# A grouped 3x3 convolution over normalised images: its beginning rearranged, and other work put between two PSUM writes

## The chip, the cores and the metric

The kernel runs on one core of a Trainium2 chip. The metric is the device time of one execution in microseconds (us): 1001.97 us before the change, the median of three runs that lay between 1000.68 and 1002.7 us.

The engines have short names in the profile. PE is TensorE (matrix products, results in PSUM), and PEld is its loading of weights. DVE is VectorE, ACT is ScalarE, POOL is GpSimd, and SP is the engine that issues most of the transfers. [...]

## The reference

The input `x` holds 160 images of 128 channels and 32 x 32 points in float32. There are five sets of weights, and each serves 32 of the images. Cut to what matters, the reference is:

```python
beta, alpha = jnp.max(U), jnp.min(U)
s1 = (beta - alpha) / 3.0
v1 = s1 * floor(U / s1)
s2 = s1 / 5.0
v2 = s2 * floor((U - v1) / s2)
w = (v1 + v2).reshape(128 * 5, 128, 3, 3)        # two-step quantised weights
g = _gn(x)                                       # 32 groups of 4 channels, per image
act = conv(g.reshape(32, 640, 32, 32), w, stride 1, pad 1, groups = 5)
return x + act.reshape(160, 128, 32, 32)
```

So every image needs a mean and a variance over each group of four channels, a normalised copy, a 3 x 3 convolution with quantised weights of its set, and the addition of the image itself.

## The kernel before

**One image is one step of the main loop** (`for i in range(self.imgs)` in `Main.run`), in which `conv(i)` is PE's part. A float32 image is represented by a high and a low float16 part, so that PE can work in float16. The 3 x 3 taps are split into three columns, worked in the order `COLS = (1, 0, 2)`. Rows are worked in pairs: the products of the sum and of the difference of two rows (`sums_of_pairs`) go to a PSUM tile `m`, of which there is only one, and the result rows to one of two PSUM tiles `eo`.

**The path of one image through the engines.** `measure(k, stages)` takes the sums (stage 0, line 192) and squares (stage 1, line 199) of an image that comes some ten to fifteen steps later; ACT does it, two passes an image, and for a few images (`by_vector`) DVE does it with `bn_stats` (line 182). When a group of images is measured, `means`, `deviations`, `variances`, `deviation` and `scales` turn that into factors, through two tiny PE products, small ACT copies and a chain on POOL. Images up to 6, and all even ones, are prepared by `normalise` and `high_part` on ACT (tiles `z`, `hi`; lines 510 and 518), `low_part` on DVE (`lo`, line 573) and `combinations` on DVE (`rows`, lines 587 to 590). The odd ones from 7 on are "combined": `outer_rows` on POOL and `combine` on DVE (tile `v`, lines 549 to 555) come first, `high_combined` on ACT (`vh`, line 560) and `low_combined` on DVE (`vl`, line 566) after that.

**Around one product of PE.** In `conv(i)`, PE first writes `m` for image i+1 (12 products if i+1 is combined, 6 if not), then the rest of image i into its `eo` tile. After the products into `m`, `leave(i+1)` copies one half of `m` to SBUF on ACT (line 708), and `pairs(i+1)` writes the sum (line 717) and then the difference (line 718) of the two halves into a fresh `eo`, both on DVE. Only when line 718 has read `m` may PE write `m` for the next image. `residual` (line 732) takes a finished `eo` out by ACT, and an accumulating transfer adds it to the image.

**The order of each engine's queue is written out by hand**: it is the order of the calls in `run`. The weights of the next set are quantised meanwhile in small steps on DVE: a generator `later`, of 14 instructions a column and three columns a set, from which `take(later, 1)` draws one instruction at a time; in an even step two are drawn (one after `low_part`, one after `pairs`), in an odd step one (after `low_combined`, ahead of `pairs`). A finished column is transposed by PE, and ACT makes `wt` and `half` of it (`keep_column`, lines 475 and 476).

**Ahead of the loop** stand the range of the weights, the quantising of the first set by columns (`first`, `second`, `third`), the statistics of images 0 to 7, and the direct products of images 0 to 2 (`direct_hi`, `direct_lo`, line 613), which don't use row pairs. `warm_up` gives PE ten products of zeros (line 631) while it waits.

**How far measuring runs ahead**: at step i, images up to `i + min(10 + i // 2, 15)` are measured. DVE measures the images 8, 10, 12, 14, 16 and 18.

Of the kernel before, what the change touches and what calls it, by code (L numbers as in the profile page):

```python
# [132 lines left out]
def run(steps):  # L133

    while True:
        try:
            next(steps)
        except StopIteration as end:
            return end.value
# [170 lines left out]
class Main:  # L310
# [24 lines left out]
    STAT_LEAD = 14  # L335
    LOAD_LEAD = 20
    STEADY = 7
    MEASURED = 20
    EARLY = 8
    FIRST = 3  # L340

# [4 lines left out]
    def __init__(self, tc, ctx, keep, x, u, out):  # L346
        nc = self.nc = tc.nc
        self.imgs, C, self.H, self.W = x.shape
        P = self.P = nc.NUM_PARTITIONS
        assert C == P and self.H * self.W == 1024  # L350
        self.per_set = self.imgs // N_SETS
        self.xv = x.rearrange("(b n) c h w -> n c b (h w)", n=N_SETS)
        self.ov = out.rearrange("(b n) c h w -> n c b (h w)", n=N_SETS)
        self.uv = u.rearrange("n (o i k) -> n o i k", o=C, k=TAPS)

        def pool(name, bufs, **kw):
            return ctx.enter_context(tc.tile_pool(name=name, bufs=bufs, **kw))

        self.const = pool("const", 1)
        self.qpool = pool("quant", 1)  # L360
        self.wpool = pool("weights", 2)
        self.upool = pool("u", 1)
        self.xpool = pool("x", 12)
        self.zpool = pool("z", 3)
        self.parts = pool("parts", 5)
        self.rows = pool("rows", 4)
        self.wide = pool("wide", 1)
        self.wide_parts = pool("wide_parts", 2)
        self.evac = pool("evac", 2)
        self.sums = pool("sums", 4)  # L370
        self.unread = pool("unread", 1)
        self.small = pool("small", 3)
        self.ps_eo = pool("ps_eo", 2, space=PSUM)
        self.ps_m = pool("ps_m", 1, space=PSUM)
        self.ps_stat = pool("ps_stat", 1, space=PSUM)
        self.ps_tr = pool("ps_tr", 1, space=PSUM)
        self.steps = Steps(nc, keep)
        self.chunks, self.z, self.hi, self.v, self.eo, self.m = {}, {}, {}, {}, {}, {}
        self.sum = {}
        self.wts = {}  # L380
        self.columns = []

        cuts = [0, 2, 4, 8, 12, *range(16, self.imgs + 1, 8)]
        self.groups = [range(a, b) for a, b in zip(cuts, cuts[1:])]
        self.group_of = {i: k for k, g in enumerate(self.groups) for i in g}
        self.stats = {}
# [95 lines left out]


    def by_vector(self, i):
        return self.EARLY <= i < self.MEASURED and i % 2 == 0

    def measure(self, i, stages=(0, 1)):

# [91 lines left out]
    def combinations(self, i):  # L580


        nc, P, H, W = self.nc, self.P, self.H, self.W
        lo = self.los[i % len(self.los)]
        rows = self.v[i] = self.rows.tile([P, 2048], MM, tag="rows", name=f"rows{i}")
        d, st = self.halves(rows)
        nc.vector.tensor_sub(d, lo[:, 0:H, :], lo[:, 2 : H + 2, :])
        pairs = lo[:, 1 : H + 1, :].rearrange("p (i a) w -> p a i w", a=2)
        nc.vector.tensor_add(st[:, 0], pairs[:, 0], pairs[:, 1])
        nc.vector.tensor_sub(st[:, 1], pairs[:, 1], pairs[:, 0])  # L590

    def halves(self, v):

# [28 lines left out]
    def banks(self, pool, tag, i):  # L622
        return pool.tile([self.P, 2, self.H // 2, self.W], F32, tag=tag, name=f"{tag}{i}")

    def warm_up(self):


        zeros = self.los[3].rearrange("p h w -> p (h w)")
        target = self.banks(self.ps_m, "m", "warm")
        for _ in range(10):  # L630
            self.nc.tensor.matmul(
                target[:, 0].rearrange("p i w -> p (i w)"), zeros[:, :128], zeros[:, :512],
                start=True, stop=True,
            )

    def direct_hi(self, i, col):
# [39 lines left out]
    def conv(self, i, on_the_way):  # L676


        if self.FIRST < i < self.imgs - 1:
            self.sums_of_pairs(i + 1)  # L680

        for halves in ((0,), (1,)) if i == self.imgs - 1 else ((0, 1),):
            for col in self.COLS:
                if col == self.COLS[1] and i == self.FIRST:
                    self.sums_of_pairs(i + 1)
                if col != self.COLS[0] and halves[-1] == 1:
                    on_the_way(col)
                self.rest_of_column(i, col, halves)
        del self.v[i]
# [18 lines left out]
        self.nc.scalar.copy(m2, self.m[i][:, 1])  # L708
        self.m[i] = self.m[i], m2

    def pairs(self, i):

        nc = self.nc
        m, m2 = self.m.pop(i)
        eo = self.eo[i] = self.banks(self.ps_eo, "eo", i)
        rows = eo.rearrange("p h (i a) w -> p (h i) a w", a=2)
        nc.vector.tensor_add(rows[:, :, 0], m[:, 0], m2)  # L717
        nc.vector.tensor_sub(rows[:, :, 1], m[:, 0], m2)  # L718

    def by_hand(self, i):  # L720
# [33 lines left out]
    def run(self):  # L754
# [43 lines left out]
        def measure(stage, *images):  # L798
            for i in images:
                self.measure(i, (stage,))  # L800
# [25 lines left out]
        measure(1, 3)  # L826
        self.stats[1].means()
        self.stats[1].deviations()
        self.warm_up()
        parts(0)  # L830
        self.stats[1].variances()
        self.stats[1].deviation()
        self.stats[1].scales()
        self.normalise(1)
        run(first)
        self.high_part(1)
        parts(2)
        take(second, 2)
# [5 lines left out]

        for i in range(self.FIRST):
            self.direct_hi(i, self.COLS[0])
        self.direct_lo(0, self.COLS[0])
        self.direct_lo(1, self.COLS[0])
        measure(0, 4, 5)
        take(third, 1)  # L850
        measure(1, 4, 5)
        self.normalise(3)
        run(second)
        self.high_part(3)
        self.direct_lo(2, self.COLS[0])
        measure(0, 6, 7)
        measure(1, 6, 7)
        for i in range(self.FIRST):
# [4 lines left out]
        self.stats[2].means()  # L863
        self.stats[2].deviations()
        self.low_part(3)
        self.combinations(3)
        self.steps.choose()
        ready, middle, measured, loaded = [], [], self.EARLY, 6
        later, turned = iter(()), []
        for i in range(self.imgs):  # L870
# [27 lines left out]
            else:  # L898
                j = i - 1
                self.conv(i, on_the_way)  # L900
            ahead = i + min(10 + i // 2, self.STAT_LEAD + 1)
            to_measure = range(measured, min(self.imgs, ahead))
            measured += len(to_measure)
            if n + 1 < N_SETS:
                if b == (2 if n == 0 else 0):
                    self.load_set(n + 1)
                if b == (4 if n == 0 else 2):
                    later = (s for col in self.COLS for s in self.make_column(n + 1, col))
            by_scalar = [k for k in to_measure if not self.by_vector(k)]

            if i < self.FIRST:

                if i == self.FIRST - 1:
                    self.leave(i + 1)
                    self.pairs(i + 1)
                    self.combinations(i + 2)
                self.residual(j)
                if i == self.FIRST - 2:
                    self.low_part(i + 3)
                for k in by_scalar:  # L920
                    self.measure(k, (0,))
                self.normalise(i + 4)
                for k in by_scalar:
                    self.measure(k, (1,))
                self.high_part(i + 4)
            else:

                direct = i + 2 < self.imgs and not self.combined(i + 2)
                if self.combined(i + 2):
                    self.low_combined(i + 2)  # L930
                if direct:
                    self.low_part(i + 2)
                take(later, 1)
                if direct:
                    self.combinations(i + 2)
                if i > self.FIRST and self.by_hand(j):
                    self.residual(j)
                for k in by_scalar:
                    self.measure(k, (0,))
                if i > self.FIRST and not self.by_hand(j):  # L940
                    self.residual(j)
                    self.accumulate(j)
                if self.combined(i + 4):
                    self.outer_rows(i + 4)


                if i + 1 < self.imgs:
                    self.leave(i + 1)
                if self.combined(i + 3):
                    self.high_combined(i + 3)  # L950
                elif self.FIRST + 3 < i + 3 < self.imgs:
                    self.normalise(i + 3)
                    self.high_part(i + 3)
                for k in by_scalar:
                    self.measure(k, (1,))
            for st in middle:
# [8 lines left out]
            if i >= self.FIRST:  # L965

                if i + 1 < self.imgs:
                    self.pairs(i + 1)
                if self.combined(i + 4):
                    self.combine(i + 4)  # L970
                else:
                    take(later, 1)
                if b == self.per_set - 4:
                    run(later)

            middle, ready = ready, []
            for k in to_measure:
                if self.by_vector(k):
                    self.measure(k)
                group = self.group_of[k]  # L980
                if k + 1 == self.groups[group].stop:
                    ready.append(self.stats[group])
# [53 lines left out]
```

## Time and profile before

The span of the profiled execution is 1000.0 us. Busy times of the engines in stretches of the span:

| stretch (us) | PE | DVE | ACT |
|---|---|---|---|
| 0 to 20 | 1.60 | 14.02 | 6.26 |
| 20 to 40 | 15.09 | 19.17 | 18.45 |
| 40 to 50 | 10.00 | 9.41 | 8.48 |
| 70 to 80 | 9.57 | 9.90 | 6.51 |
| 80 to 90 | 10.00 | 9.90 | 7.05 |
| 100 to 120 | 20.00 | 18.76 | 19.69 |
| 160 to 200 | 40.00 | 38.26 | 39.62 |
| 500 to 600 | 100.00 | 95.94 | 99.12 |
| 900 to 940 | 40.00 | 34.20 | 30.49 |
| 980 to 1001 | 12.98 | 6.58 | 1.17 |

A row is read against the length of its stretch: PE at 40.00 of 40 us had no gap. "Busy" of PE comes from modelled ends, so it tells of gaps and not of PE's speed. The page names the waits by the line that waits and the line that released it, and a view of the timeline gives each instruction's start and duration, with the idle time of its engine ahead of it in square brackets.

### The profile page before, as it was taken

To read this page: it belongs to the slowest core of one execution; us is meant where nothing else is said; L and a number is where in the kernel's file an instruction comes from. 1 tells how busy PE (TensorE), PEld (TensorE's weight loads), DVE (VectorE), ACT (ScalarE), POOL (GpSimd) and SP (SyncE) were. 2 spreads that over 40 slices of the span, in tenths; PEclk is the share of its full clock that TensorE was granted. 3 is DMA by queue.
4 is the path that set the end of the run, shared out by engine and by line. 5 is a ranking of instruction groups with operands and counts; after the bars stand their busy time and mean duration, and the time that the engine had idled before them with its cause. 6 is when DMAs were issued, how large, how long until landed. Compare 5 with 4: busy or idle time off the path is not lost.

```text
span 1000.0 us, 15935 instructions
## 1 busy us (share of the span) xinstructions
PE 959.1 (96%) x5920; PEld 576.2 (58%) x5920; DVE 906.7 (91%) x1227; ACT 916.5 (92%) x1249; POOL 374.4 (37%) x567
## 2 busy tenths in 40 slices
PE   1889999999999999999999999999999999999997
PEld 1445556665666665666666566666665666666554
DVE  7989899999999999989999999999999988888884
ACT  4877999999999999999999999999999999998560
POOL 3523164353515143625243443515243523233310
PEclk9899999999999999999999999999999999999999
DMA  9638789999999999999999999999999999997773
GB/s 365 239 105 232 196 220 262 280 262 274 287 272 264 261 273 265 267 275 281 273 279 263 260 270 269 293 276 277 268 253 264 281 282 262 274 244 196 192 179 141
DMA packets 67287, 254.42 MB, mean 254 GB/s; under 512 B 5248, under 2 KB 5248, under 8 KB 67200
## 3 DMA queue, kind: packets, MB, share of 16 engines
q1 hardware_dynamic: 45168, 173.09, 50.5%
q0 software_dynamic: 22032, 80.23, 41.2%
q8 instruction: 48, 0.79, 0.3%
q14 instruction: 39, 0.32, 0.1%
HBM read 89.19 MB, written 83.89 MB: 173 GB/s over the span
## 4 chain that ended last, share of the span: by engine, by line
PE 82%; DVE 8%; ACT 6%; issue 2%; DMA 1%; POOL 1%; SPq 0%; DVEq 0%; ACTq 0%
PE eo L613 27%; PE m L650 27%; PE eo L650 27%; ACT junk L199 2%; ACT vh L560 1%; ACT sum L732 1%; PE m L613 1%; DVE lo L573 1%; DVE eo L717 1%; DVE eo L718 1%; ACT m L708 1%; ACT z L510 1%; DVE vl L566 1%; DVE st L182 1%; DMA range<-in_L_conv_U_dram 1%
## 5 line engine op out<-in xcount | busy, mean ns | idle before, releaser
L650 PEld LDWEIGHTS <-wt 128*128 128x128 f16 x4212 | 410.8, 98 | 238.5 <-DVE eo L718 9.2
L613 PE MATMUL eo<-hi,wt 128*128 128x496 f16 (+1 forms) x1476 | 355.0, 377 | 4.6 <-DVE eo L718 3.3
L745 POOL DMA_DIRECT2D xt<-sum x153 | 135.9, 888 | 456.2 <-ACT sum L732 440.0
L613 PEld LDWEIGHTS <-wt 128*128 128x128 f16 x1548 | 152.1, 100 | 151.1 <-DVE eo L718 3.8
L566 DVE SCALAR_TENSOR_TENSOR vl<-v,rstd,vh 128x2048 f16<-128x2048 f32 x77 | 180.8, 2347 | 3.1 <-ACT vh L560 3.1
L650 PE MATMUL m<-vh,wt 128*128 128x496 f16 (+1 forms) x462 | 175.5, 380 | 5.9 <-DVE eo L718 5.9
L650 PE MATMUL eo<-vl,wt 128*128 128x256 f16 (+1 forms) x924 | 177.1, 273 | 0.0
L650 PE MATMUL eo<-vh,wt 128*128 128x256 f16 (+1 forms) x924 | 177.1, 273 | 0.0
L199 ACT ACTIVATE junk<-xt,mv 128x1024 f16<-128x1024 f32 x154 | 176.3, 1145 | 0.3
L192 ACT ACTIVATE junk<-xt 128x1024 f16<-128x1024 f32 x154 | 162.7, 1057 | 14.0 <-DMA xt<-in_x_dram 10.9
L650 PE MATMUL m<-vl,wt 128*128 128x496 f16 (+1 forms) x462 | 175.4, 380 | 0.0
L732 ACT ACTIVATE sum<-eo 128x1024 f32<-128x1024 f32 x153 | 154.2, 1008 | 16.6 <-PE eo L650 16.6
L717 DVE TENSOR_TENSOR eo<-m,m 128x512 f32<-128x512 f32 x157 | 109.0, 694 | 61.2 <-ACT m L708 60.8
L560 ACT ACTIVATE vh<-v,rstd 128x2048 f16<-128x2048 f32 x77 | 155.0, 2013 | 0.3 <-DVE v L555 0.3
L650 PE MATMUL eo<-rows,wt 128*128 128x248 f16 (+1 forms) x960 | 144.3, 273 | 0.0
L650 PE MATMUL m<-rows,wt 128*128 128x496 f16 (+1 forms) x480 | 116.9, 380 | 1.4 <-DVE eo L718 1.3
L718 DVE TENSOR_TENSOR eo<-m,m 128x512 f32<-128x512 f32 x157 | 109.8, 699 | 5.4
L708 ACT COPY m<-m 128x512 f32<-128x512 f32 x157 | 91.2, 581 | 25.3 <-PE m L650 22.4
L510 ACT ACTIVATE z<-xt,shift,rstd 128x1024 f32<-128x1024 f32 x83 | 103.2, 1244 | 2.6 <-POOL shift L242 2.6
L573 DVE TENSOR_TENSOR lo<-z,hi 128x1024 f16<-128x1024 f32 x83 | 101.6, 1224 | 1.8 <-ACT hi L518 1.8
L518 ACT CAST hi<-z 128x1024 f16<-128x1024 f32 x83 | 86.8, 1045 | 2.5
L549 DVE TENSOR_TENSOR v<-xt 128x960 f32<-128x960 f32 x77 | 88.5, 1150 | 0.0
(111 smaller groups left out, 824.8 us busy)
## 6 DMA issues: line engine op xcount, KB each, us to landing
xt<-in_x_dram SPq DMA_DIRECT2D x78, 1024.0 KB, 8.9
out_dram<-xt SPq DMA_DIRECT2D x78, 1024.0 KB, 5.1
xt<-sum POOLq DMA_DIRECT2D x153, 512.0 KB, 6.8
range<-in_L_conv_U_dram SPq DMA_DIRECT2D x4, 576.0 KB, 7.1
u<-in_L_conv_U_dram SPq DMA_DIRECT2D x4, 576.0 KB, 11.5
xt<-in_x_dram SPq DMA_DIRECT2D x4, 512.0 KB, 10.5
out_dram<-xt SPq DMA_DIRECT2D x3, 512.0 KB, 2.7
u<-in_L_conv_U_dram SPq DMA_DIRECT2D x2, 288.0 KB, 3.1
```

What stands on the lines that cost most here:

```text
L192: self.nc.scalar.activation(junk, image, ACTF.Copy, scale=-1.0 / image.shape[1], accum_out=self.mv[:, j, 0:1],)
L199: self.nc.scalar.activation(junk, image, ACTF.Square, bias=self.mv[:, j, 0:1], accum_out=self.mv[:, j, 1:2],)
L510: nc.scalar.activation(z, self.image(i), ACTF.Identity, bias=st.shift[:, j : j + 1], scale=st.rstd[:, j : j + 1],)
L560: self.nc.scalar.mul(vh, self.v[i], st.rstd[:, j])
L566: self.nc.vector.scalar_tensor_tensor(vl, self.v[i], st.rstd[:, j], self.hi[i], ALU.mult, ALU.subtract)
L573: self.nc.vector.tensor_sub(lo[:, 1 : self.H + 1, :].rearrange("p h w -> p (h w)"), self.z.pop(i), self.hi[i].rearrange("p h w -> p (h w)"),)
L613: nc.tensor.matmul(target[:, h, r0 - h0 : r1 - h0, c0:c1], self.wts[n, col][:, k, :], tile[:, s0 : s0 + r1 - r0, c0 + dw : c1 + dw], start ...
L650: self.nc.tensor.matmul(target[:, :, c0:c1], self.wts[n, col][:, kind, :], source[:, :, c0 + dw : c1 + dw], start=start, stop=stop, skip_g ...
L717: nc.vector.tensor_add(rows[:, :, 0], m[:, 0], m2)
L718: nc.vector.tensor_sub(rows[:, :, 1], m[:, 0], m2)
L732: nc.scalar.mul(self.sum[i], eo, 0.5)
L745: self.nc.gpsimd.dma_start(self.image(i), self.sum.pop(i), accum_op=ALU.add)
```

## The change

It rearranges the beginning and two places of the main loop.

- **Zeros.** `warm_up` takes a count; it gives 14 products of zeros where it gave 10, and 7 more after the first column's transposes, so that PE's products follow each other up to the first real one.
- **Ahead of the loop.** `direct_lo(2)` comes ahead of the statistics of images 4 and 5; the weights of the second column are kept ahead of the second stage of image 5 and of `normalise(3)`.
- **Steps 0 to 2.** DVE measures images 8, 10 and 11 at places written out by hand, ACT image 9. `pairs(3)` comes ahead of `low_part(4)` and its combinations. In step 3, `sums_of_pairs(4)` comes ahead of the third column instead of the second.
- **Lead.** Measuring runs ahead by `10 + i // 4`, still up to 15. The groups of statistics get shorter ([16, 20) and [20, 24) instead of [16, 24)), and DVE measures 8, 10, 11, 14, 20 and 26.
- **Between the PSUM writes.** `pairs` calls `between()` after line 717: in an even step the third instruction of `combinations`, in an odd step one instruction of `later`, which was drawn ahead of `pairs` before.

```diff
-    MEASURED = 20
+    MEASURED = 32
...
-        cuts = [0, 2, 4, 8, 12, *range(16, self.imgs + 1, 8)]
+        cuts = [0, 2, 4, 8, 12, 16, 20, *range(24, self.imgs + 1, 8)]
...
     def by_vector(self, i):
-        return self.EARLY <= i < self.MEASURED and i % 2 == 0
+        return i in (8, 10, 11) or self.EARLY <= i < self.MEASURED and i % 6 == 2
...
-                if col == self.COLS[1] and i == self.FIRST:
+                if col == self.COLS[2] and i == self.FIRST:
                     self.sums_of_pairs(i + 1)
...
-    def pairs(self, i):
+    def pairs(self, i, between=lambda: None):
...
         nc.vector.tensor_add(rows[:, :, 0], m[:, 0], m2)
+        between()
         nc.vector.tensor_sub(rows[:, :, 1], m[:, 0], m2)
...
-        self.warm_up()
+        self.warm_up(14)
         parts(0)
...
         run(first)
+        self.warm_up(7)
         self.high_part(1)
...
-        self.direct_lo(0, self.COLS[0])
-        self.direct_lo(1, self.COLS[0])
+        for i in range(self.FIRST):
+            self.direct_lo(i, self.COLS[0])
         measure(0, 4, 5)
         take(third, 1)
-        measure(1, 4, 5)
-        self.normalise(3)
+        measure(1, 4)
         run(second)
-        self.high_part(3)
-        self.direct_lo(2, self.COLS[0])
+        measure(1, 5)
+        parts(3)
...
-            ahead = i + min(10 + i // 2, self.STAT_LEAD + 1)
+            ahead = i + min(10 + i // 4, self.STAT_LEAD + 1)
...
-                if i == self.FIRST - 1:
-                    self.leave(i + 1)
-                    self.pairs(i + 1)
-                    self.combinations(i + 2)
+                if i == 0:
+                    measure(0, 8, 9, 10)
+                    self.normalise(4)
+                    self.high_part(4)
+                if i == 2:
+                    self.leave(3)
+                    self.normalise(5)
+                    measure(1, 9)
+                    self.high_part(5)
+                    self.pairs(3)
+                    self.low_part(4)
+                    run(self.combinations(4))
                 self.residual(j)
...
+                if i == 1:
+                    measure(0, 11)
             else:
...
+                elif i + 2 < self.imgs:
                     self.low_part(i + 2)
-                take(later, 1)
-                if direct:
-                    self.combinations(i + 2)
+                    take(later, 1)
+                    rows = self.combinations(i + 2)
+                    take(rows, 2)
...
-                    self.pairs(i + 1)
+                    self.pairs(i + 1, lambda: take(rows if i % 2 == 0 else later, 1))
+                run(rows)
...
+            if i >= self.FIRST:
+                measure(0, *by_vector)
             for k in to_measure:
-                if self.by_vector(k):
-                    self.measure(k)
```

More of the change, by code (lines that the diff above doesn't have):

```diff
@@ L586, in combinations @@
         d, st = self.halves(rows)
-        nc.vector.tensor_sub(d, lo[:, 0:H, :], lo[:, 2 : H + 2, :])
+        yield nc.vector.tensor_sub(d, lo[:, 0:H, :], lo[:, 2 : H + 2, :])
         pairs = lo[:, 1 : H + 1, :].rearrange("p (i a) w -> p a i w", a=2)
-        nc.vector.tensor_add(st[:, 0], pairs[:, 0], pairs[:, 1])
-        nc.vector.tensor_sub(st[:, 1], pairs[:, 1], pairs[:, 0])
+        yield nc.vector.tensor_add(st[:, 0], pairs[:, 0], pairs[:, 1])
+        yield nc.vector.tensor_sub(st[:, 1], pairs[:, 1], pairs[:, 0])
     def halves(self, v):
@@ L623, in banks, with warm_up @@
         return pool.tile([self.P, 2, self.H // 2, self.W], F32, tag=tag, name=f"{tag}{i}")
-    def warm_up(self):
+    def warm_up(self, count):
         zeros = self.los[3].rearrange("p h w -> p (h w)")
-        target = self.banks(self.ps_m, "m", "warm")
-        for _ in range(10):
+        if "warm" not in self.m:
+            self.m["warm"] = self.banks(self.ps_m, "m", "warm")
+        for _ in range(count):
             self.nc.tensor.matmul(
-                target[:, 0].rearrange("p i w -> p (i w)"), zeros[:, :128], zeros[:, :512],
-                start=True, stop=True,
+                self.m["warm"][:, 0].rearrange("p i w -> p (i w)"), zeros[:, :128],
+                zeros[:, :512], start=True, stop=True,
             )
@@ L865, in run @@
         self.low_part(3)
-        self.combinations(3)
+        run(self.combinations(3))
         self.steps.choose()
@@ L909, in run @@
             by_scalar = [k for k in to_measure if not self.by_vector(k)]
+            by_vector = [k for k in to_measure if self.by_vector(k)]
             if i < self.FIRST:
-                if i == self.FIRST - 1:
-                    self.leave(i + 1)
-                    self.pairs(i + 1)
-                    self.combinations(i + 2)
-                self.residual(j)
[L918 to L925, printed above, removed]
+                if i == 0:
[10 more added lines that the diff above has]
+                    run(self.combinations(4))
+                self.residual(j)
+                if i == 1:
+                    measure(0, 11)
             else:
-                direct = i + 2 < self.imgs and not self.combined(i + 2)
+                rows = iter(())
                 if self.combined(i + 2):
                     self.low_combined(i + 2)
-                if direct:
+                elif i + 2 < self.imgs:
                     self.low_part(i + 2)
-                take(later, 1)
-                if direct:
-                    self.combinations(i + 2)
+                    take(later, 1)
+                    rows = self.combinations(i + 2)
+                    take(rows, 2)
                 if i > self.FIRST and self.by_hand(j):
@@ L944, in run @@
                     self.outer_rows(i + 4)
+                part = i + 3 < self.imgs and not self.combined(i + 3)
                 if i + 1 < self.imgs:
                     self.leave(i + 1)
+                if part:
+                    self.normalise(i + 3)
+                    self.high_part(i + 3)
                 if self.combined(i + 3):
                     self.high_combined(i + 3)
-                elif self.FIRST + 3 < i + 3 < self.imgs:
-                    self.normalise(i + 3)
-                    self.high_part(i + 3)
                 for k in by_scalar:
```

## Prediction

> **What bounds the kernel now.** I read the busy times by stretch first, then PE's timeline, then ACT's waits, then one steady step on three engines.
>
> ```profile
> 50.00:60.00 10.00, 9.11 (x43) 3.96 (x41) 6.41 (x13) 6.43 (x9) 4.28 (x13) 1.00 0.00 1
> 60.00:70.00 10.00, 6.73 (x38) 3.67 (x38) 9.69 (x21) 9.69 (x17) 1.31 (x4) 1.00 0.42 139
> ...
> 90.00:100.00 10.00, 8.01 (x51) 4.65 (x50) 9.86 (x17) 8.92 (x14) 3.49 (x7) 1.00 0.91 263
> ...
> 120.00:140.00 20.00, 17.97 (x114) 10.74 (x113) 17.33 (x24) 18.64 (x30) 13.00 (x16) 1.00 0.88 245
> ...
> 300.00:400.00 100.00, 100.00 (x629) 60.86 (x628) 95.34 (x128) 98.93 (x136) 38.34 (x60) 1.00 0.99 266
> ```
>
> Columns: stretch, length, busy time of PE, weight load, DVE, ACT, POOL, then PE's clock and the DMA. PE has holes only ahead of 160 us (and 0.6 us near 231); from 300 to 900 us it has none. But ACT is as full: its missing 1.07 us of 100 are gaps between instructions. The waits of ACT, from 34 to 165 us, and then from 165 to 900 us (the last line):
>
> ```profile
> ACT m L708 <- PE m L650: 4.1, 4, 1.7
> ACT sum L732 <- PE eo L650: 3.3, 4, 1.4
> ACT ve L231 <- PE pg L225: 2.8, 1, 2.8
> ACT z L510 <- POOL shift L242: 2.1, 2, 1.3
> ACT wt L475 <- PE pt L462: 0.9, 1, 0.9
> ACT ngm L217 <- PE pg L208: 0.5, 1, 0.5
> ACT vh L560 <- DVE v L555: 0.3, 1, 0.3
> ...
> ACT m L708 <- PE m L650: 0.4, 2, 0.3
> ```
>
> Early, ACT idles 14.0 us; later it waits 0.4 us in 735. So after the beginning two engines run level, and **a gain of PE lasts only if ACT gets as far ahead**. PE's own losses:
>
> ```profile
> 30.49 5.20 PE L613 MATMUL eo<-hi,wt 128*128 128x512 f16 x12 [1.35 <-ACT wt L475]
> ...
> 62.40 1.44 PE L613 MATMUL eo<-hi,wt 128*128 128x512 f16 x6 [3.30 <-DVE eo L718]
> ...
> 70.43 1.47 PE L650 MATMUL m<-rows,wt 128*128 128x512 f16 x6 [1.29 <-DVE eo L718]
> ...
> 97.66 0.39 PE L650 MATMUL m<-vh,wt 128*128 128x512 f16 x1 [1.92 <-DVE eo L718]
> ```
>
> In the first line 12 products take 4.99 us to the next start, 0.416 each; warm ones take 1.27 / 6 = 0.212. About 14 run slow, which costs 14 x 0.204 = 2.9 us. Last, one odd step in steady state (ACT, DVE, PE):
>
> ```profile
> 369.94 0.59 ACT L708 COPY m<-m 128x512 f32<-128x512 f32 x1
> ...
> 369.37 0.77 DVE L108 SCALAR_TENSOR_TENSOR tt<-nn,s1nhi,u 128x384 f32<-128x384 int16 x1
> 370.56 0.70 DVE L717 TENSOR_TENSOR eo<-m,m 128x512 f32<-128x512 f32 x1 [0.42 <-ACT m L708]
> 371.30 0.70 DVE L718 TENSOR_TENSOR eo<-m,m 128x512 f32<-128x512 f32 x1
> ...
> 372.54 0.38 PE L650 MATMUL m<-vh,wt 128*128 128x512 f16 x1
> ```
>
> The instruction of `later` (L108) hides in DVE's wait for ACT. Line 718 ends at 372.00 and PE starts at 372.54, at its own pace: 0.54 us of slack. Where PE does wait, it starts 0.06 after line 718, so 0.48 is to spare. PE had three transposes of weights (0.16) to do in this step; the plain odd steps have a slack of 0.37, so 0.31 to spare. Even steps have about 1.5.
>
> [...] Here the clock was 1.00 up to 29.7 us, 0.50 to 36.5 and 1.00 from there on, steps of 6.8 us[...]. [...]PE must wait for line 718, as the releasers above show. [...]line 718 starts 0.73 after 717, while the instruction after 718 starts 0.61 after it. That is all the new `between` can win: 0.11 us of DVE, which isn't the bound.
>
> **The change part by part.**
>
> *Zeros.* 14 products from 23.51: 6.5 slow ones to about 26.3, the rest warm, end near 27.9. The variances (28.34) and transposes (to 29.14) follow, then 7 x 0.212 = 1.5 warm (3.0 if slow): the first real product at 30.63 instead of 30.49, but warm. High parts 0 and 1 end at 33.2; then PE waits for `hi` of image 2, ACT's at 34.6. It reaches the second column's transposes at 39.8 as before, since their quantised values come from DVE at 39.57 and DVE was full from 20 to 49. So the 2.9 us end in that wait.
>
> *Ahead of the loop.* With `normalise(3)` moved back, `wt` follows the transposes at 40.35 instead of 40.99, and PE starts 0.6 earlier. But ACT now stands idle from 38.67 to 40.35, where it did `normalise(3)`, and its queue ends 1.5 later. `wt` of the third column comes at 49.35 instead of 48.40, the POOL chain 1 us later, and `ve` of images 4 to 7 at 53.7 instead of 52.73.
>
> *Steps 0 to 3.* DVE's statistics of 8 and 10 fill 50.5 to 54.1 (1.8 each, from lines 182 to 186), that of 11 ends at 59.1, and `pairs(3)` at 60.5. conv(3) starts at 60.55 instead of 62.40. `sums_of_pairs(4)` ends at 65.4, and with leave, pairs and combinations that of image 5 starts at 67.65 instead of 70.43. ACT waits 2.5 for `leave(4)`.
>
> *Lead and groups.* With less to measure per step, the hole at 97.66 goes: I get 92.95. Carried on with the same durations, image 13 starts at 118.7 instead of 123.43, 4.7 us ahead. But by step 20 both versions have measured up to image 34, six by DVE: **ACT has the same work by then**. Its idle time from `ve` to `leave(22)` at 181.27 was 14.0 - 4.2 (those ahead of `ve`) = 9.8. In the replay it is 8.0 (0.8 for `shift`, 2.5 for `leave(4)`, and eight waits of 0.4 to 1.3 for PE), after a start 1.0 later. So ACT is 0.8 ahead at image 22, not 4.7, and the steps that measure two images make PE wait for `leave`: I get 158.15 instead of 160.14 for image 19, and nearly nothing at 23. The group of images 24 to 31 has one step for its POOL chain, as [16, 24) had, where `z` waited 1.3; between 0 and 1.3, I take 0.65. Left: 0.15 us.
>
> *Between the writes, even steps.* 0.33 us moves behind line 717; line 718 comes no later. Nothing.
>
> *Between the writes, odd steps.* Line 718 comes later by the instruction's issue distance less 0.11: 0.53 for L108 (0.64), 0.42 for L109 and L110 (0.53), 0.36 for L111 (0.47), 0.16 for L112 (0.27), 0.56 for L125 (0.67), 0.22 to 0.30 for L99. Nothing hides it, because `leave` starts right after PE's products. In the second set of weights the odd steps draw L109, L112, L108, L111, L99, L110, L125, L109, L112, L108, L111, L99, L110. To spare, read off the timeline step by step (PE's start less the end of line 718, less 0.06), they have 0.46, 0.31, 0.31, 0.31, 0.62, then 0.06 (a column was just kept), 0.31, 0.31, 0.46, 0.48, 0 (kept again), 0.31, 0.45; the lag after a kept column is caught up by PE's own wait, so I count it once. PE waits 0, 0, 0.22, 0.05, 0, 0.36, 0.25, 0.11, 0, 0.05, 0.36, 0, 0: **1.4 us a set**. Sets three and four show the same slacks: 3 x 1.4 = 4.2. In the first set ACT is late anyway, and the insertion shifts PE by at most 0.3 once. The fifth set has none left to quantise. Without the 0.11 it is 2.3 a set, 7.0 in all.
>
> Sum: 1002.0 - 0.15 + 0.3 + 4.2 = **1006.3 us**.
>
> **The rivals.**
>
> - *The beginning counts and the insertion is hidden*: the 4.7 us of image 13 last, 1002.0 - 4.7 = 997.3. For it: PE has 13 us of holes and cold products. Against it: ACT's 0.4 us of waiting, and the slack of 0.37. It needs ACT to find 4 us more than I count. 0.25.
> - *Both count*: 1002.0 - 4.7 + 4.2 = 1001.5, no change. For it: my replay of ACT's idle time may be off by 2 to 4 us. 0.17.
> - *My forecast*, 1006.3: 0.48.
> - *The clock falls again.* [...] In the window that ended at 29.7 about half busy was followed by slow products, but the hole at 58.9 to 62.4 was not. One slow period of 6.8 us costs up to 3.4 more: about 1009. 0.10.
>
> **The numbers.** Faster 0.25, same 0.17, slower 0.58. The range reaches from 997.5, nearly the first rival, to 1009, the last one[...].
>
> **What would show it.** The insertion: PE's waits on line 718 after 240 us, absent before, 0.2 to 0.4 each in odd steps, worst for L125, L108 and after kept columns, and none after 800. The beginning: first real products at 0.21 us, then a wait near 33; image 13's products near 119, image 23's near 183. ACT's idle time ahead of 182 us near 9 from 53.7. Wrong if PE stays without gaps from 240 to 900, or if image 23 starts over 2 us ahead of 183.69.

## The result and the profile after

The changed kernel took **1009.34 us** (median of six executions, 1006.61 to 1011.6) beside 1002.27 us before: a ratio of 1.007, 95% interval 1.0051 to 1.0088. The forecast, 1006.3, had the direction and missed 3 us; 1009.34 lies just above its range. The profiled execution spans 1007.6 us, 7.6 more than before.

In the changed kernel the sum of `pairs` is line 719 (717 before), the difference 721 (718), `leave` 709 (708), the products of row pairs 651 (650), `residual` 735 (732) and the zeros 632 (631).

First the busy times by stretch, as before (PE, weight load, DVE, ACT, POOL, then PE's clock and the DMA):

```profile
50.00:60.00 10.00, 8.77 (x44) 4.05 (x43) 8.42 (x25) 5.81 (x12) 4.79 (x14) 1.00 0.00 1
60.00:70.00 10.00, 9.04 (x50) 4.48 (x49) 9.86 (x16) 7.12 (x10) 0.00 (x0) 1.00 0.41 127
90.00:100.00 10.00, 10.00 (x66) 6.15 (x65) 8.47 (x14) 9.81 (x16) 6.63 (x12) 1.00 0.83 220
120.00:140.00 20.00, 18.73 (x115) 10.82 (x114) 17.31 (x27) 19.20 (x30) 8.04 (x14) 1.00 0.95 265
160.00:164.00 4.00, 4.00 (x13) 1.48 (x11) 4.00 (x7) 3.09 (x6) 0.67 (x1) 0.59 1.02 288
300.00:400.00 100.00, 99.65 (x626) 60.14 (x624) 92.45 (x126) 98.32 (x136) 46.83 (x59) 1.00 0.99 268
```

PE has filled its holes at 60 to 70 and 90 to 100 us. But it is no longer at 100.00 in 300 to 400, and **from 160 to 164 its clock is 0.59**: a fall that before doesn't have there.

PE's timeline at the places of the prediction:

```profile
31.63 2.74 PE L613 MATMUL eo<-hi,wt 128*128 128x512 f16 x12
35.80 0.38 PE L613 MATMUL m<-hi,wt 128*128 128x512 f16 x1 [1.43 <-ACT hi L518]
...
61.44 1.44 PE L613 MATMUL eo<-hi,wt 128*128 128x512 f16 x6 [0.50 <-DVE eo L721]
...
68.63 1.47 PE L651 MATMUL m<-rows,wt 128*128 128x512 f16 x6 [0.46 <-DVE eo L721]
```

The first twelve products take 2.74 us where they took 5.20: warm from the first. The 1.43 ahead of the next one is the wait for image 2's high part in which that gain ends. The waits of 3.30 and 1.29 for `pairs` have shrunk to 0.50 and 0.46.

ACT's waits, from 34 to 165 us, and after the "..." from 165 to 900:

```profile
ACT m L709 <- PE m L651: 5.0, 5, 2.9
ACT ve L231 <- PE pg L225: 4.0, 2, 3.4
ACT z L510 <- POOL shift L242: 2.7, 3, 1.3
ACT wt L475 <- PE pt L462: 1.6, 1, 1.6
ACT vh L560 <- POOL v L539: 1.0, 1, 1.0
ACT sum L735 <- PE eo L651: 1.0, 2, 0.5
...
ACT m L709 <- PE m L651: 2.7, 12, 0.3
ACT vh L560 <- POOL v L539: 0.6, 1, 0.6
ACT sum L735 <- PE eo L651: 0.5, 1, 0.5
```

Early ACT idles 15.3 us, not less than the 14.0 before, so it has not got ahead. Later it waits 3.8 us where it waited 0.4: now it follows a PE that is held up. Who holds PE, from 240 to 900 us, in a view that had no line before:

```profile
PE m L651 <- DVE eo L721: 1.3, 4, 0.8
```

The view lists only the longer waits; the short ones are seen step by step. Here is the step that the prediction showed, now with L108 between the writes:

```profile
374.34 0.59 ACT L709 COPY m<-m 128x512 f32<-128x512 f32 x1
...
374.96 0.70 DVE L719 TENSOR_TENSOR eo<-m,m 128x512 f32<-128x512 f32 x1 [1.08 <-ACT m L709]
...
375.57 0.73 DVE L108 SCALAR_TENSOR_TENSOR tt<-nn,s1nhi,u 128x384 f32<-128x384 int16 x1
...
376.22 0.69 DVE L721 TENSOR_TENSOR eo<-m,m 128x512 f32<-128x512 f32 x1
...
376.97 0.39 PE L651 MATMUL m<-vh,wt 128*128 128x512 f16 x1
```

The second write starts 1.26 after the first (0.74 before), so 0.52 later; the prediction had 0.53. It ends at 376.91, and PE starts 0.06 after it: the slack of 0.54 is used up to the 0.06 that PE takes anyway.

**PE's starts side by side** (the first product into `m` of each image, after less before) show where the 7.6 us come from: image 13 starts 4.32 us earlier, image 18 (153.17) 3.04 earlier, image 19 (159.62) only 0.52 earlier, and image 20 (169.03) 1.04 *later*. At image 23 it is 3.07 late, at image 29 3.6, at 357 us 4.4, at 568 us 5.6, and from 780 us on 7.62 to the end. So 6.1 us go between images 18 and 23, where the prediction had a gain of 2 to 3 us given back and nothing more. This is that place, on four engines:

```profile
145.08 5.23 POOL L538 TENSOR_SCALAR v<-xt,ngm 128x32 f32<-128x32 f32 x1
145.36 5.21 POOL L539 TENSOR_SCALAR v<-xt,ngm 128x32 f32<-128x32 f32 x1
...
150.60 2.00 ACT L560 ACTIVATE vh<-v,rstd 128x2048 f16<-128x2048 f32 x1 [1.04 <-POOL v L539]
...
157.61 0.70 DVE L719 TENSOR_TENSOR eo<-m,m 128x512 f32<-128x512 f32 x1 [2.62 <-ACT m L709]
158.22 0.73 DVE L125 SCALAR_TENSOR_TENSOR rest<-k,s1n,u 128x384 f32<-128x384 f16 x1
158.87 0.69 DVE L721 TENSOR_TENSOR eo<-m,m 128x512 f32<-128x512 f32 x1
...
159.62 0.39 PE L651 MATMUL m<-vh,wt 128*128 128x512 f16 x1 [2.36 <-DVE eo L721]
...
160.71 0.61 PE L651 MATMUL m<-vl,wt 128*128 128x496 f16 x1
161.11 0.63 PE L651 MATMUL m<-vh,wt 128*128 128x512 f16 x1
```

Read it downwards. Two tiny operations on POOL (32 columns each) last 5.2 us; ACT's `vh` waits for them; everything behind it on ACT comes later, `leave` included, so DVE waits 2.62 for it; L125 stands between the writes; PE stands still for 2.36 us. From 160.71 products take 0.43 us to the next start instead of 0.22, for 3.4 us by the clock's records. That is 3.4 / 2 = 1.7 us.

### The profile page after: what moved, and what is told of

Its sections match the earlier page's. It is cut to its first block, busy times and chain, and to the rows that moved or that the text cites. A ratio compares the mean times of both kernels' runs of the same rounds, so it can differ in the third digit from the quotient of the medians.

```text
span 1007.6 us, 15974 instructions
## 1 busy us (share of the span) xinstructions
PE 964.1 (96%) x5935; PEld 575.3 (57%) x5935; DVE 892.9 (89%) x1227; ACT 918.4 (91%) x1251; POOL 406.8 (40%) x575
## 4 chain that ended last, share of the span: by engine, by line
PE 71%; ACT 14%; DVE 6%; issue 4%; POOL 3%; DMA 1%; SPq 0%; POOLq 0%; DVEq 0%; ACTq 0%
PE eo L613 24%; PE m L651 24%; PE eo L651 22%; ACT junk L199 4%; ACT vh L560 2%; ACT sum L735 2%; ACT m L709 2%; ACT z L510 2%; ACT junk L192 1%; DVE eo L719 1%; DVE eo L721 1%; POOL v L538 1%; DMA range<-in_L_conv_U_dram 1%; ACT hi L518 1%; DVE ext L421 1%
```

## The experiments

Times are medians, ratios to the kernel before with their 95% intervals. All diffs but those of e1, e5 and e7 are against the changed kernel.

**e1: the odd insertion alone, in the kernel before.**

```diff
-                take(later, 1)
+                if direct:
+                    take(later, 1)
...
-                    self.pairs(i + 1)
+                    self.pairs(i + 1, lambda: take(later, i % 2))
```

> The kernel before with one part of the change: in odd steps one instruction of later stands between the two PSUM writes instead of ahead of them. My theory (what stands between delays line 718 and so PE, by more than its slack): PE waits 1.0 to 1.4 us in each of sets 2 to 4, on the instructions L108, L125 and after kept columns, and up to 0.7 in the first set where ACT is late: 1005.5 to 1007 us against 1002.3 before. Rival (the loss comes from the rearranged beginning, the insertion is hidden in steady state): within 0.5 us of before.

1007.69 us, 1.0049 (1.0035 to 1.0062), 0.7 above the expected range. In its trace PE falls behind by 1.1 to 1.2 us in each of sets two to four. In the first set it loses 2.5, but not by the insertion alone: in this execution the clock was 0.50 from 61.7 to 68.5 us, in and after the old hole near 60, and 1.6 of the 2.5 are there at image 4, ahead of the first step with an insertion.

**e2: the change without the odd insertion.**

```diff
-                    self.pairs(i + 1, lambda: take(rows if i % 2 == 0 else later, 1))
+                    if i % 2:
+                        take(later, 1)
+                    self.pairs(i + 1, lambda: take(rows, 1))
```

> The changed kernel with the odd steps' instruction of later put back ahead of the two PSUM writes; all the rest of the change stays. My theory (the insertion costs about 4 us, and the beginning costs some more because ACT gets no further ahead and a hole of PE lets the clock fall): 1003 to 1005.5 us, still slower than before, and no PE wait on line 718 after 240 us. Rival A (the insertion in the first set opens the hole, and without it the beginning gains): under 1001. Rival B (the beginning makes the whole loss): 1009.

1001.35 us, 0.9989 (0.9981 to 0.9998), below the 1003 to 1005.5 that were expected. Against before, PE is 4.0 us ahead at image 13, 2.26 at image 19 and 0.30 at image 23, and 0.06 behind at image 29. The gain of the new beginning is given back, as the forecast had it; whether ACT's work is the reason is asked next. No wait for line 721 is listed after 240 us.

**e4 and e6: is it ACT's work that takes the gain back?** In e4 the lead of before (`i // 2`) holds from step 3 on, with the groups of before, and DVE measures 8, 10, 11, 14, 16 and 18. In e6 the lead is the new one, and DVE measures eight images instead of six: 8, 10, 11, 14, 18, 22, 26 and 30. Both are without the odd insertion.

```diff
# e4
-            ahead = i + min(10 + i // 4, self.STAT_LEAD + 1)
+            ahead = i + min(10 + i // (2 if i >= self.FIRST else 4), self.STAT_LEAD + 1)
# e6
-        return i in (8, 10, 11) or self.EARLY <= i < self.MEASURED and i % 6 == 2
+        return i in (8, 10, 11) or self.EARLY <= i < self.MEASURED and i % 4 == 2
```

> The same as the run without the odd insertion, but from step 3 on measuring runs ahead by 10 + i // 2 again, with the groups of statistics of the kernel before, and DVE measures 8, 10, 11, 14, 16 and 18. My theory (ACT has the same work by image 34 whichever way it is spread, so the lead alone moves the end by little): within 1.5 us of the run without the odd insertion. Rival (the slower lead puts the steps with two images measured late, behind each other, and that is what costs): faster than it by 2 to 4 us, near 1000.

> The same as the run without the odd insertion, but DVE measures 8, 10, 11, 14, 18, 22, 26 and 30, eight images instead of six (20 goes to ACT, 18, 22 and 30 come from it). My theory (ACT sets the pace of the beginning once the first images are through): ACT has 4.9 us less to do before image 35, DVE 3.5 more, and the end comes 2 to 5 us earlier than in the run without the odd insertion, 999 to 1002. Rival (PE or DVE sets it): no earlier, or later by 1 to 3 us because DVE gets late.

e4: 1000.02 us, 0.9974 (0.9966 to 0.9982), 1.3 below e2. e6: 999.51 us, 0.9973 (0.9962 to 0.9983), 1.8 below e2. In the traces PE ends 2.3 and 2.6 us ahead of e2; but the first product of e4 starts 0.85 earlier than that of e2 (17.63 against 18.48), which leaves it 1.5. In e6, two passes on ACT taken over by DVE for two images are worth 2 x (1.06 + 1.15 + 0.38) = 5.2 us of ACT, and a third to a half of it comes out at the end. In e4 ACT has as much to measure up to image 34 as in e2, and still there is a gain: how the work is spread counts as well as its amount.

**f1: the changed kernel once more**, beside f2, f3 and e7.

> The changed kernel as it is, once more with a profile. If what the first profile of it shows in the first set belongs to the kernel (a 2.4 us hole of PE near 159 us, then a stretch at half clock, and rows of v on POOL that take 5 us), the hole and the halved clock are there again, PE is 3 to 4 us behind the kernel without the odd insertion at image 29, and the median is 1008 to 1010. If they were chance, PE is about 0.5 us behind it at image 29, and the median lies near 1006.

1006.63 us (1006.36 to 1007.52, five executions), 1.0046 (1.0033 to 1.0059). PE has the same hole (2.37 us, up to 158.84), but in the profiled execution the clock stays at 1.00.

**f2 and f3: the odd insertion from the second set on, and in the first set only.**

```diff
# f2
+                    if i % 2 and i < 32:
+                        take(later, 1)
+                    self.pairs(i + 1, lambda: take(rows if i % 2 == 0 else later, i % 2 == 0 or i >= 32))
# f3
+                    if i % 2 and i >= 32:
+                        take(later, 1)
+                    self.pairs(i + 1, lambda: take(rows if i % 2 == 0 else later, i % 2 == 0 or i < 32))
```

> The changed kernel with the odd insertion only from step 32 on; below, the instruction of later stands ahead of the two writes. My theory (in sets 2 to 4 the insertion costs 1.1 us each and some more where rows of v come late): 3.5 to 4.5 us above the kernel without any odd insertion, 1005 to 1006, with its PE starts equal to that kernel's up to image 31. Rival (the cost needs the state that the first set leaves): under 1003.5.

> The changed kernel with the odd insertion only below step 32. My prediction had 0.3 us for it, the first profile shows 3.6. If the first set is where my sum was short: 1004 to 1005.5, 3 to 4 us above the kernel without the odd insertion, with a hole of PE over 1.5 us between 150 and 165 us and half clock after it. If the prediction's term was right and the profile a chance: 1001.5 to 1002.5.

f2: 1004.25 us, 1.0021 (1.0011 to 1.0031), 2.9 above e2; in the trace 1.15 us in each of the three sets. f3: 1003.38 us, 1.0013 (1.0005 to 1.0021), 2.0 above e2, and 1.5 in the traces. Both cost less than was expected of them, 3.5 to 4.5 and 3 to 4. But against the prediction **the first set costs 2.0 us where the forecast had at most 0.3**, and the three others 2.9 where it had 4.2.

**e7: a double dose.** In the kernel before, two operations of 128x384 float32 on a tile of their own stand between the writes in the odd steps from 33 on. `later`'s instruction stays ahead of the writes.

```diff
+    def filler(self):
+        for _ in range(2):
+            self.nc.vector.tensor_sub(self.fill, self.fill, self.fill)
...
-                    self.pairs(i + 1)
+                    self.pairs(i + 1, (lambda: self.filler()) if i % 2 and i > 32 else (lambda: None))
```

> The kernel before with two useless DVE subtractions (128 x 384, float32, about 0.47 us each) between the two PSUM writes of every odd step from 33 on. My theory (PE waits for delay less slack): line 718 comes 0.94 - 0.11 = 0.83 later, 0.31 of it is hidden in plain odd steps and 0.45 in those with two statistics products, so 0.52 or 0.38 in each of 61 odd steps: 26 to 31 us, 1028 to 1034. Rival (PE has other slack, or DVE's gain between the writes is larger): under 1015.

1039.72 us, 1.0373 (1.0355 to 1.0391). Each operation took 0.53 us and not the 0.47 of the expectation, so the second write came 1.67 after the first instead of 0.73: 0.94 later. PE loses 38.0 us over 63 odd steps (the expectation counted 61), 0.60 each; with 0.31 to spare in a plain step the rule gives 0.94 - 0.31 = 0.63, and 0.49 where 0.45 is to spare. The rule "delay less slack" holds; the price of the filler was wrong. PE's waits, from 240 to 900 us (line 719 is the second write here):

```profile
PE m L650 <- DVE eo L719: 22.6, 50, 1.2
```

**f4 and h1: one step of the first set.** What f3 and the changed kernel share, and e2 and f2 don't, is POOL's 5.2 us in step 15. f4 is f3, and h1 the whole change, with L110 of that one step drawn ahead of the sum again.

```diff
# h1
+                    if i == 15:
+                        take(later, 1)
-                    self.pairs(i + 1, lambda: take(rows if i % 2 == 0 else later, 1))
+                    self.pairs(i + 1, lambda: take(rows if i % 2 == 0 else later, i != 15))
```

> The odd insertion only in the first set, and there not in step 15, where L110 is drawn ahead of the sum again. Theory (in step 15 the insertion closes the gap in DVE's queue, and POOL's rows of v for image 19, lines 538 and 539, then take 5.2 us instead of 1.2): the two rows take 1.2 us again, ACT's vh doesn't wait, PE's hole near 159 us falls from 2.37 to about 1.2 (what L125 adds there stays), and the median lies about 1.2 us below the 1003.4 of the kernel with all of the first set, near 1002.2. Rival (the first set loses because leave comes late in many odd steps, and POOL's long rows are only a symptom): the rows stay at 5.2 us or the hole stays near 2.4, and the time stays at 1003.4 within 0.4.

> The changed kernel with one instruction moved: in step 15 L110 is drawn ahead of the sum instead of between the writes. Theory: the hole near 159 us is about 1.2 instead of 2.37; the mean granted clock is 0.998 or more in nearly all executions (a fall of 3.4 us at half clock would show as 0.997 or less, as in 4 of 11 executions of the changed kernel); 1006.6 less 1.2 = 1005.4, and no execution above 1007. Rival (the clock falls for another reason than this hole, or PE's loss comes back later): executions at 0.997 are as frequent as before and the median stays at 1006.6 or above.

f4: 1001.80 us, 0.9998 (0.999 to 1.0007): 1.6 below f3 and 0.45 above e2. h1: 1006.08 us (1005.44 to 1006.58), 1.0042 (1.0028 to 1.0055). The timeline of h1, POOL and PE:

```profile
144.89 1.21 POOL L538 TENSOR_SCALAR v<-xt,ngm 128x32 f32<-128x32 f32 x1
146.09 1.22 POOL L539 TENSOR_SCALAR v<-xt,ngm 128x32 f32<-128x32 f32 x1
...
157.97 0.39 PE L651 MATMUL m<-vh,wt 128*128 128x512 f16 x1 [1.22 <-DVE eo L721]
```

and its busy times, the same columns as above:

```profile
160.00:164.00 4.00, 4.00 (x25) 2.19 (x24) 4.00 (x8) 4.00 (x6) 0.88 (x1) 1.00 1.00 314
```

POOL is back at 1.2 us each, `vh` doesn't wait, and half of the hole is gone. Against f1, h1 gains 0.55 us in the medians, not the 1.2 expected (0.9 in the traces near 286 us). The median of h1 stands 0.2 from the forecast of the whole change.

**The clock, execution by execution.** Each execution has a mean granted clock. The last 1.8 to 4.7 us of every profile are at half clock (4.3 us before, 3.8 in the changed kernel); that alone leaves 0.998 or 0.999. A further period of 3.4 us at half clock lowers it by 3.4 x 0.5 / 1007 = 0.0017. So I take 0.998 and more for no such period, and 0.997 or less for at least one:

| kernel | PE's hole near 159 us | at 0.998 or more | at 0.997 or less |
|---|---|---|---|
| changed (11 executions, f1 included) | 2.4 | 7, median 1006.63 | 4: 1007.52, 1009.32, 1009.35, 1011.6 |
| f3 | 2.4 | 9, median 1003.19 | 4, median 1004.49 |
| e2 | 0.64 | 12 | 1 |
| f2 | 0.56 | 9 | 0 |
| f4 | 1.1 | 13, median 1001.8 | 0 |
| h1 | 1.2 | 5, median 1006.08 | 0 |

With the long hole the clock fell in 8 of 24 executions, without it in 1 of 40. Of the kernels that the table leaves out, e6 (no hole above 1.2 us after 34 us) fell in 0 of 8 executions, g1 (1.8) in 1 of 10, and e4 (2.02) in 5 of 15. In f3 the four that fell are the four slowest, 1.3 us above the others. In the first six executions of the changed kernel three fell, and a fourth (1010.1 at 0.999) was as slow without a fall; so their median is 1009.3. Of the five of f1 one fell. That fourth execution isn't explained by the clock.

**e5: the zeros alone, in the kernel before.**

```diff
-        self.warm_up()
+        self.warm_up(14)
         parts(0)
...
         run(first)
+        self.warm_up(7)
```

> The kernel before with the zeros' products alone (14 and 7). Theory (the 2.9 us of slow products end in PE's wait for hi of image 2): first real products at 0.21 us each, a new wait of 1 to 1.5 us near 34, and the time within 1 us of before. Rival (a warm PE carries its 2.9 us on): 999.5.

1002.70 us, 1.0002 (0.9994 to 1.0011). PE's timeline:

```profile
31.04 2.74 PE L613 MATMUL eo<-hi,wt 128*128 128x512 f16 x12
35.23 1.01 PE L613 MATMUL m<-hi,wt 128*128 128x512 f16 x4 [1.45 <-ACT hi L518]
```

Warm products, then 1.45 us of waiting: nothing is won.

**g1: a try at the best of both**, e4's lead with two more images (20 and 22) measured by DVE.

```diff
-        return i in (8, 10, 11, 14, 16, 18)
+        return i in (8, 10, 11, 14, 16, 18, 20, 22)    # against e4
```

> The change without the odd insertion, with the lead of i // 2 and the groups of before, and DVE measuring 8, 10, 11, 14, 16, 18, 20 and 22. If ACT's amount of work sets the pace of the beginning, the two gains of 2.3 to 2.6 us (old lead; more images measured by DVE) add in part: 998 to 999.5, below both kernels. Rival (DVE has no room left in steps that have both a statistic and the quantising of the second set): 1000 or more.

999.82 us, 0.9978 (0.9968 to 0.9987): below both kernels, but no better than e4 or e6. The two gains don't add. PE still has a hole of 1.8 us at 95.4, as e4 has, ahead of the places where the two extra images count; what else holds it wasn't tried.

## Why the prediction was off, point by point

**Zeros: right.** A first warm product, a wait for image 2, nothing left; e5 shows it alone.

**The beginning: right in size, its reason only in part.** Image 13 was forecast at 118.7 and came at 119.11; the products that stood at 70.43 before were forecast at 67.65 and came at 68.63 (the whole profile starts its first product 1.1 us later than before, at 19.03 instead of 17.89, when the weights' range arrives). The 4 us are gone by image 29, as e2 shows; e2's median is 1 us below before, where the forecast had 0.15. That ACT's work takes them is supported by e6, where less of it gains 1.8 us. But "the same work by then" isn't the whole reason: e4 has the same work too and keeps 1.3 us more, so the new, slower lead with its groups costs some of what the beginning wins. For the change as it stands, the rivals that let 4.7 us of the beginning last fall.

**Even steps: no sign against them.** They were not run alone; e2 holds them, and with the whole beginning it is 1 us below before.

**Odd steps of sets two to four: right, a little dear.** Forecast 4.2. The traces give 1.1, 1.1 and 1.8 us for the three sets of the changed kernel, together 4.0, and 3.4 in f1 and f2; the medians 2.9 (f2 less e2) and 4.3 (h1 less f4). What varies is one step near 765 us: there too POOL's rows of `v` took 3.4 us in the changed kernel and in h1, ACT's `vh` waited 0.6, and PE 0.8; in f1 PE waited 0.14.

**The first set: the step that failed.** It read "the insertion shifts PE by at most 0.3 once", because ACT was late anyway; the first set cost 2.0 us (f3 less e2). For all of the first set's odd steps but one that is what was measured: f4 less e2 is 0.45 in the medians and 0.3 in the traces. Step 15 costs 1.6 more in the medians of f3 and f4, 0.55 in those of f1 and h1, and 0.9 to 1.2 in their traces. The price of an insertion was taken from PE's and DVE's timelines, and POOL was left out. With one DVE instruction moved by 0.7 us, two short operations of POOL lasted 5.2 us instead of 1.2, and ACT, which the whole beginning waits for, waited for them.

**The clock: a rival, put at the wrong place.** "One slow period of 6.8 us costs up to 3.4 more" had a chance of 0.10, at the wait near 33. There the clock held at 1.00, as it did from 20 us on. It fell at 161 us, after the hole that step 15 had opened, for 3.4 us and 1.7 us of loss, and by its mean in a third of the executions. The forecast asked this of the one new wait that it had foreseen, and not which holes the insertion would open. The old hole that it named as harmless (59.1 to 62.4 by its line) was so in the profiles of before and e5, but the clock fell in the same hole in e1 and e7.

**The sum.** Measured once more (f1) the changed kernel came to 1006.63 us, and without step 15 (h1) to 1006.08; the forecast was 1006.3. That they lie so close to it is in part luck, because errors cancel: the beginning gave about 0.8 more than forecast (e2), the first set took 1.7 more, and sets two to four took up to 1.3 less. What the first profile, with 1007.6 us, has more than that of f1 (1004.6) is the clock's 1.7 us and a start later by 0.7 (at image 4, 65.00 against 64.27), 2.4 of the 3.0; the rest is that step near 765. This accounts for the profiled execution. Why the first six have a median 2.7 above f1's is in part open: a fall of the clock is worth 1.3 us in f3's medians, and one of the four slow executions had none.

## What to carry to other kernels

When an instruction is moved by half a microsecond in one queue, follow all engines that work at that time, the idle ones too: an engine that is 40% busy (POOL here) can hand the delay to the one that isn't. A slack read step by step priced the steady state well here (delay less slack: 4.2 us forecast, 4.0 in the traces of the changed kernel); in the beginning, where each engine had just enough, one single step cost more than the others together (1.6 us against 0.45, f3, f4 and e2). And ask of each hole that a change opens whether the clock will hold through it: where it falls only in some executions (4 of 11 here), a median of few executions can jump.

## What the runs showed of the hardware

**Two short operations on POOL lasted 5.2 us, until DVE had begun line 719.** Lines 538 and 539 (128x32 float32) took 0.28 us at best, and 5.2 us in step 15 of the changed kernel, f1 and f3. There line 538 starts 0.2 us ahead of DVE's line 549 and line 539 0.06 us after it, and they end 0.14 and 0.4 us after DVE has begun line 719, the next write to `eo`. On DVE, in the changed kernel:

```profile
145.30 1.14 DVE L549 TENSOR_TENSOR v<-xt 128x960 f32<-128x960 f32 x1
...
150.17 0.69 DVE L719 TENSOR_TENSOR eo<-m,m 128x512 f32<-128x512 f32 x1
```

In e2, f4 and h1, where line 538 starts 0.1 us behind line 549, both take 1.2 us beside the same operations of DVE. They start earlier in the changed kernel (145.08, and 145.37 in e2) because POOL's line 239 ahead of them ends earlier: at 143.82, and at 144.11 in e2, in both 0.2 us after DVE began its sum (line 719), which e2 does only after L110. What held the two operations for 5.2 us is not shown by any run; only the effect of moving L110 is, from 5.2 us to 1.2.

**The clock fell after windows of 3.41 us in which PE had little to do.** The times at which the clock changes lie on one grid of 3.41 us: before, 29.69, 36.52 and 995.66 us are 2.00 and 281.00 steps apart; in the changed kernel, 160.72, 164.13 and 1003.81 are 1.00 and 246.00 apart. Against the span's start the grid differs from run to run: its first point lies at 0.3, 3.2, 0.3, 1.2 and 2.4 us in the five profiles below, in their order. Five windows between 34 and 960 us, of the changed kernel, f1, e1, e7 and the kernel before (PE's busy time follows the length; the clock is the last number but two):

```profile
157.31:160.72 3.41, 1.10 (x6) 0.52 (x7) 3.11 (x5) 3.38 (x4) 1.95 (x3) 1.00 0.68 129
...
156.80:160.21 3.41, 1.36 (x7) 0.66 (x8) 3.38 (x5) 3.35 (x6) 1.78 (x3) 1.00 0.76 144
...
58.30:61.71 3.41, 1.30 (x7) 0.39 (x4) 3.06 (x7) 3.38 (x5) 0.00 (x0) 1.00 0.00 0
...
120.71:124.12 3.41, 1.39 (x12) 0.94 (x11) 1.64 (x3) 3.38 (x6) 1.44 (x3) 1.00 0.81 268
...
60.41:63.83 3.42, 1.43 (x8) 0.74 (x9) 3.31 (x10) 3.42 (x5) 0.00 (x0) 1.00 0.00 0
```

In the window after it, the clock was 0.50 in the changed kernel, in e1 and in e7, and 1.00 in f1 and before. A second window of e7, from 59.27 with 0.36 us busy, was followed by 0.50 too. All other windows in that stretch that ran at full clock had 1.49 us of work or more before, 1.69 or more in the changed kernel, and were followed by 1.00. So my estimate from these windows is a limit near 1.4 of 3.41 us, about 40% busy, to the accuracy of PE's modelled ends (1.39 was followed by 0.50, and 1.36 by 1.00). It is one for this stretch alone: ahead of it, before's window from 26.28 to 29.69 had 1.71 us of work and was followed by 0.50 as well. The estimate agrees with the same hole of 2.37 us lowering the clock in one profile and not in the other: in f1 0.33 us of it fell into the window before. From these figures I estimate that about 2.0 us of a hole had to lie in one window, which a hole of 2.37 does in (3.41 + 2.37 - 2 x 2.0) / 3.41 = about half of all positions, and one of 2.02 in (3.41 + 2.02 - 2 x 2.0) / 3.41 = 0.42; 8 of 24 and 5 of 15 executions were seen.
